# Score matmuls of two softmax passes mixed in half quads, and softmax sums inverted as [128, 32] through DRAM

## The chip, the cores and the metric

The kernel is one program on one core of a Trainium2 chip. The core has five engines that run side by side, each through its own list of instructions in order: PE (TensorE) multiplies matrices out of the on-chip memory SBUF into eight PSUM banks of [128, 512] float32; DVE (VectorE), ACT (ScalarE) and POOL (GpSimd) work elementwise; SP (SyncE) here only issues DMAs. Engines wait for each other by semaphores. The metric is the time of one execution in microseconds (us) of device time. Three runs of the kernel before took 2528.41, 2529.75 and 2535.48 us, median 2529.75. One further execution was profiled; it took 2526.84 us, of which the profile's span covers 2525.1 us.

## The reference

Four batches of 1024 tokens, 256 wide, pass through six layers in float32: a mixture of experts, a causal softmax attention with 16 heads of 16, the mixture again, a feed-forward with 4-bit rounding, a linear attention, and the feed-forward again. The change lies in the softmax attention alone:

```
q, k, v  = split heads of layernorm(x) @ W_qkv.T          # 4 batches, 16 heads, [1024, 16] each
attn     = softmax(where(j <= i, q_i . k_j / 4, -inf))     # over keys j
x        = x + (attn @ v) @ W_o.T
```

The kernel computes each row's softmax in two passes: a first one finds the row's largest score, a second one computes the scores again with that maximum taken off, exponentiates them, and multiplies them by the values and by a column of ones, which gives the sum to divide by.

## The kernel before

The stage is softmax_phase, from about 380 to 1262 us of the span. It works in 16 groups of four heads (n = 0 to 15; four groups for each batch). The four heads of a group lie in four strips of 32 partitions, so that a score matmul uses 32 of PE's 128 rows and four heads can run at the same time; such a set of four is called a quad here. Each float32 matmul shows as two PE instructions in the trace, so a quad is x8.

softmax_exponentials (L822) holds a group's loop: 12 steps, 4 for the first 512 queries (qb = 0) and 8 for the second (qb = 1). Because of the causal mask the widths of the steps are 512, 384, 256, 128, then four times 512, then 512, 384, 256, 128. A step of group n does, in PE's order:

- S: a quad of transposed scores (L866) from keys kT and from less, the queries with the maximum in a spare row; ACT turns each bank into exponentials (L877, two heads to a tile ex), and on the masked steps POOL clears the upper triangle (L880).
- other work that others holds, taken out by some(): the next batch's norm, values and projections, the output projection of the batch before (L724), the transposes for less (L818, softmax_shift), the division by the sums (softmax_quotients), and in groups 13 to 15 the router of the next layer.
- M: a quad of the maxima pass for the NEXT group n + 1 (L789); DVE reduces each of its four banks, with tensor_reduce where nothing is masked (L798), else with a masked reduction (L801, into low).
- P: the products of the exponentials of the step BEFORE with the values (L836), four matmuls into one bank acc. After the last step of a block of 512 queries DVE copies acc to ys (L845), and two DMAs on SP's queue (L851) bring the numerators to yT and the sums to den, where each sum already stands in 16 equal rows.

The matmuls of S and M, and most of the other work, take their banks in turn from a pool of 7 (bank, L96); acc has the eighth bank. A matmul therefore waits until the bank that was handed out seven takes earlier has been read, by ACT if it held S, by DVE if it held M. PE's order is that of the code (manual_schedule). The orders of DVE, ACT, POOL and SP are set when the program is built, by a scheduler with estimated durations; each engine then keeps its order, so an instruction that waits holds up all behind it.

The division (softmax_quotients, L706) works on blocks of eight heads by 512 queries, of which there are 16: four reciprocals of [128, 128] of den (L712), each followed by a multiply (L713). For qb = 0 they are put into others in the middle of an odd group (late), for qb = 1 in the even group that follows. SP's queue carries, in this stage, the spreads of projected queries and keys (L770), the two DMAs of L851 and the router's stores (L351).

## Time and profile before

| what | value |
|---|---|
| median of three runs | 2529.75 us |
| profiled execution, span | 2526.84 us, 2525.1 us |
| busy: PE, DVE, ACT, POOL over the span | 90%, 69%, 40%, 26% |
| softmax groups 0 to 15 | 449.2 to 1250.7 us, 801.5 us |
| in them busy: PE, DVE, ACT, POOL | 771.5, 568.9, 373.7, 123.2 us |
| granted PE clock in them, by group | 0.82 to 1.00 |
| one step's quads at 512 wide: S, M, P | 0.96 to 1.07 us, the same, 1.00 us from start to the next start |
| four reductions of M at 512 wide (DVE) | 2.48 us |
| four exponentials of S at 512 wide (ACT) | 2.06 us |
| reciprocal [128, 128], x64 | 930 ns mean, 57.9 us |
| multiply [128, 128], x64 | 227 to 293 ns |

A busy PE is not a PE at its peak: matmuls are recorded from their issue to a modelled end, and a quad of which one member is late counts as busy throughout. So the distance from one quad's start to the next one's start is read from the timeline instead. A group's beginning is the start of its first S matmul; the groups last 42.2 to 66.5 us, the last one, which has no M, 30.7 us. In a wait line, "A <- B: t, k, m" says that A's engine sat idle for t us in all, k times, at most m us, until B had finished.

### The profile page before, as it was taken

How to read it: one execution, taken by the hardware profiler on the slowest of the kernel's cores; microseconds unless marked ns; L12 is line 12 of the kernel's file. 1: busy time of each engine (PE TensorE's matmuls, PEld its weight loads, DVE VectorE, ACT ScalarE, POOL GpSimd, SP SyncE). 2: the span in 40 equal slices, each digit the busy share in tenths (PEclk: the TensorE clock that was granted, in tenths of full speed). 3: DMA queues.
4: the chain of work that ended last, by engine and by line, in shares of the span. 5: the costliest groups of instructions: out<-in, count | busy, mean ns of one | idle time of the engine just before them, and what ended most of it. 6: DMA issues, size and time to landing. Idle time of an engine off the chain costs nothing. (4 is left out here: it accounts for less than half of the span.)

```text
span 2525.1 us, 36840 instructions
## 1 busy us (share of the span) xinstructions
PE 2274.6 (90%) x13313; PEld 1484.8 (59%) x13313; DVE 1737.0 (69%) x4753; ACT 1004.1 (40%) x2056; POOL 648.8 (26%) x772
## 2 busy tenths in 40 slices
PE   6799995999999999999869999589887999889988
PEld 5688883443343343343458888366665777656666
DVE  6456655776776786767533323799987888788886
ACT  3223331444444444443422322355542333345552
POOL 0345441211221111111134442222214444201111
PEclk9999997999999999998879999799998999989999
DMA  5333321101101011010033331110000000000000
GB/s 168 100 120 114 113 65 46 37 15 30 32 24 30 24 36 30 14 51 9 30 119 115 104 111 49 34 36 28 9 1 1 2 2 2 1 5 16 15 15 19
DMA packets 61950, 111.90 MB, mean 44 GB/s; under 512 B 15209, under 2 KB 42377, under 8 KB 56649
## 3 DMA queue, kind: packets, MB, share of 16 engines
q0 software_dynamic: 12192, 58.21, 7.3%
q1 hardware_dynamic: 47800, 46.74, 6.4%
q10 hardware_dynamic: 1776, 4.61, 0.5%
q8 instruction: 105, 1.72, 0.3%
q14 instruction: 77, 0.62, 0.1%
HBM read 70.21 MB, written 22.54 MB: 37 GB/s over the span
## 5 line engine op out<-in xcount | busy, mean ns | idle before, releaser
L877 ACT ACTIVATE ex<-bank 128x512 f32<-128x512 f32 (+3 forms) x768 | 317.7, 496 | 405.1 <-PE bank L866 398.3
L789 PE MATMUL bank<-kT,qT 32*128 32x512 f32 (+3 forms) x1536 | 281.7, 564 | 15.8 <-DMA qT<-qk 6.1
L880 POOL TENSOR_SCALAR_AFFINE_SELECT ex<-ex 128x256 f32<-128x256 f32 x256 | 103.9, 411 | 713.9 <-ACT ex L877 709.6
L568 PE MATMUL acc<-wf,gT 128*128 128x256 f32 x1184 | 261.8, 379 | 0.0
L568 PEld LDWEIGHTS acc<-wf,gT 128*128 128x128 f32 x1184 | 225.3, 190 | 30.2
L866 PE MATMUL bank<-less,kT 32*128 32x512 f32 (+3 forms) x1536 | 223.5, 557 | 16.8 <-DVE low L801 14.2
L574 DVE TENSOR_TENSOR y<-acc,xg 128x256 f32<-128x256 f32 x74 | 28.0, 419 | 303.7 <-issue 198.0
L1141 POOL TENSOR_TENSOR hq<-hv,ham 128x704 f32<-128x704 f32 x64 | 92.4, 1444 | 515.9 <-DVE std L1102 369.7
L798 DVE TENSOR_REDUCE part<-bank 128x1 f32<-128x512 f32 x256 | 160.3, 683 | 87.3 <-PE bank L789 87.3
L1193 PE MATMUL acc<-wdT,hqT 128*128 128x256 f32 x768 | 183.2, 390 | 35.0 <-DVE x L1195 33.7
L789 PEld LDWEIGHTS bank<-kT,qT 32*128 32x128 f32 x1536 | 127.8, 195 | 111.2 <-issue 45.9
L1193 PEld LDWEIGHTS acc<-wdT,hqT 128*128 128x128 f32 x768 | 146.6, 194 | 74.0 <-issue 47.4
L836 PE MATMUL acc<-ex,va 128*32 128x512 f32 (+3 forms) x1536 | 171.9, 529 | 1.1 <-DVE ys L845 0.9
L1163 PE MATMUL pairA<-wgT,xqT 128*128 128x352 f32 x512 | 169.9, 477 | 1.5 <-ACT xqT L1152 1.3
L552 PE MATMUL pairA<-xgT,w 128*128 128x256 f32 x608 | 162.4, 390 | 9.4 <-ACT xgT L542 8.7
L866 PEld LDWEIGHTS bank<-less,kT 32*128 32x128 f32 x1536 | 84.1, 195 | 145.8 <-issue 78.9
L1163 PE MATMUL pairB<-wuT,xqT 128*128 128x352 f32 x512 | 162.2, 460 | 0.4 <-DVE h L1177 0.4
L552 PE MATMUL pairB<-xgT,w 128*128 128x256 f32 x608 | 158.5, 384 | 0.0
L801 DVE CUSTOM_DVE_ANT_0 seen<-bank,mask_q,part 128x128 bf16<-128x128 f32 (+3 forms) x256 | 126.3, 547 | 36.4 <-PE bank L789 35.9
L559 ACT ACTIVATE gT<-pairA,b1s 128x256 f32<-128x256 f32 x152 | 72.0, 473 | 170.5 <-PE pairA L552 170.5
L552 PEld LDWEIGHTS pairA<-xgT,w 128*128 128x128 f32 x608 | 108.6, 192 | 37.9 <-ACT xgT L542 15.4
L801 DVE CUSTOM_DVE_ANT_0 seen<-bank,mask_q 128x128 bf16<-128x128 f32 (+3 forms) x256 | 110.9, 483 | 27.8 <-PE bank L789 24.5
(261 smaller groups left out, 4153.3 us busy)
## 6 DMA issues: line engine op xcount, KB each, us to landing
y_d<-y SPq DMA_DIRECT2D x36, 256.0 KB, 2.1
xn_d<-xn SPq DMA_DIRECT2D x16, 512.0 KB, 2.9
x<-in_x SPq DMA_DIRECT2D x8, 512.0 KB, 10.5
kT<-qk SPq DMA_DIRECT2D x32, 128.0 KB, 2.3
qT<-qk SPq DMA_DIRECT2D x32, 128.0 KB, 2.5
yT<-ys SPq DMA_DIRECT2D x32, 128.0 KB, 2.7
den<-ys SPq DMA_DIRECT2D x32, 128.0 KB, 2.9
out<-x SPq DMA_DIRECT2D x32, 128.0 KB, 1.7
```

The source lines that it names most:

```text
L552: nc.tensor.matmul(pg[:, f, :], lhsT=w1[:, k * FF + fc * P : k * FF + (fc + 1) * P], rhs=xgT[:, k, :], start=(k == 0), stop=(k == KD - 1),)
L568: nc.tensor.matmul(po[j], lhsT=gT[fc][:, bass.ts(j, P)], rhs=wf0[:, fc, :], start=(fc == 0), stop=(fc == NF - 1))
L789: nc.tensor.matmul(pss[h][:, 0:cols], lhsT=qT[rows, bass.ts(qt, P)], rhs=kT[rows, c * BLK : c * BLK + cols], start=True, stop=True,)
L798: nc.vector.tensor_reduce(parts[i][:, h : h + 1], pss[h][:, 0:cols], AX.X, ALU.max, negate=True)
L801: nc.vector.tensor_tensor_reduce(out=seen[:, 0:cols], in0=pss[h][:, 0:cols], in1=mask_q[:, BLK - cols : BLK], scale=-1.0, scalar=parts[i][ ...
L836: nc.tensor.matmul(acc[qb][bass.ts(h, 32), c0:BLK], lhsT=va[:, kt, NG * g + h, :], rhs=exs[h // 2][:, h % 2, c0:BLK], start=(kt == 0), sto ...
L866: nc.tensor.matmul(pss[h][:, c0:BLK], lhsT=kT[rows, bass.ts(kt, P)], rhs=held["less", n, qb][rows, c0:BLK], start=True, stop=True,)
L877: nc.scalar.activation(ex[:, j, c0:BLK], pss[2 * a + j][:, c0:BLK], AF.Exp, scale=0.25)
L880: nc.gpsimd.affine_select(out=ex[:, :, c0 : c0 + P], in_=ex[:, :, c0 : c0 + P], compare_op=ALU.is_ge, fill=0.0, base=0, pattern=[[0, 2], [ ...
L1141: nc.gpsimd.tensor_tensor(blocks_of(held["hq", p][:, j]), v[:, s], am[:, s].unsqueeze(2).to_broadcast([P, n, QB]), ALU.mult)
L1163: nc.tensor.matmul(pg[:, half, 0:FIH], lhsT=held["xqT", p][:, k, j, :], rhs=w[:, k, half * FIH : (half + 1) * FIH], start=(k == 0), stop=( ...
L1193: nc.tensor.matmul(po, lhsT=hqT[:, c, :], rhs=wdT[:, c, :], start=(c == 0), stop=(c == NFI - 1))
```

## The change

Two things change, both in the softmax stage.

1. A step's eight score matmuls are issued as two half quads of four. The first holds S of heads 0 and 1 and M of heads 2 and 3, in the order S0, M2, S1, M3; the second S2, M0, S3, M1. P of the step before stands between the two halves, others behind the second. The maxima pass takes its tiles in another order (all of c = 0 first, and from the last tile to the first), so that S and M of one step have the same width. softmax_shift has fixed places, after step 1 (for this group's qb = 1) and after step 8 (for the next group's qb = 0), and nothing else is done there; others start after step 1 and are paced by a running credit. Group 15 has no next group, so its half quads hold two matmuls each.
2. For 14 of the 16 blocks the sums no longer go to den in SBUF but to a DRAM tile den_d of [8, 512]. softmax_sums reads it back as few [128, 32], takes one reciprocal, stores it to DRAM (inv_d), and reads it back eight times, one row to 16 partitions each, into rden; one multiply of [128, 512] then divides yT. In code the two steps are invert and multiply. The two blocks of the last batch's second half keep softmax_quotients.

In the program as built, SP's queue has for such a block: yT, den_d, few, inv_d, eight loads of rden. On DVE the reciprocal stands three reductions behind the copy to ys; the multiply stands five reductions behind the reciprocal in odd groups, eight in most even ones. PE's order in group 7, which has no other work, reads: three half quads, P, half quad, shift, half quad, P, two half quads, P and so on; the last P of a group stands directly behind the second half quad of its own step.

```diff
@@ -609,7 +609,7 @@
...
-                maxima = softmax_maxima(wp, 0, hb, held)
+                maxima = [lambda item=item: softmax_quad(item) for item in softmax_maxima(wp, 0, hb, held)]
...
@@ -619,14 +619,18 @@
                 maxima = []
                 if n < last:
                     maxima = softmax_maxima(wp, n + 1, 0, held) + softmax_maxima(wp, n + 1, 1, held)
-                others = [lambda: softmax_shift(wp, held, n, 1)]
+                others = []
                 if n % 2 and n + 2 <= last:
                     others.append(lambda: softmax_spread(n + 2, held))
                 if g < 2 and b + 1 < NB:
                     others.append(lambda: softmax_inputs(wp, b + 1, g, held, give_back))
+                finish = []
                 if n % 2 == 0 and n:
-                    others += softmax_quotients((n - 1) // NG, (g // 2 + 1) % 2, 1, held)
+                    others.append(inverted)
+                    first, second = softmax_sums(wp, (n - 1) // NG, (g // 2 + 1) % 2, 1, held)
+                    others.append(first)
+                    finish.append(second)
                 if b > 0 and g in (0, 2):
                     out = softmax_out(b - 1, range(2 * g, 2 * g + TPB), held)
                     others += out
@@ -636,8 +640,6 @@
                         others += [lambda v=values: next(v, None)] * (KD + TPB)
                 if n % 2 == 0 and n + 2 <= last:
                     others += softmax_project(wp, n + 2, held)
-                if n < last:
-                    others.append(lambda: softmax_shift(wp, held, n + 1, 0))
...
-                late = softmax_quotients(b, g // 2, 0, held) if g % 2 else []
+                others += finish
+                late = []
                 if n == last:
-                    late += softmax_out(b, (0, 1, 2, 3), held)
+                    late = softmax_quotients(b, 1, 0, held) + softmax_out(b, (0, 1, 2, 3), held)
+                elif g % 2:
+                    first, inverted = softmax_sums(wp, b, g // 2, 0, held)
+                    late = [first]
                 softmax_exponentials(wp, n, vas[b % 2], held, maxima, others, late)
...
+    def softmax_sums(wp, b, c, qb, held):
+        def spread(d):
+            return d.rearrange("h (r c) -> (h r) c", c=8 * BLK // P)
+        def invert():
+            inv_d = dram.tile([8, BLK], F32, tag="inv_d", name="inv_d", bufs=3)
+            few = small.tile([P, 8 * BLK // P], F32, tag="few", name="few")
+            nc.sync.dma_start(out=few, in_=spread(held["den", b, c, qb]))
+            nc.vector.reciprocal(few, few)
+            nc.sync.dma_start(out=spread(inv_d), in_=few)
+            held["rden", b, c, qb] = rden = wp.tile([P, BLK], F32, tag="den", name="den", bufs=3)
+            for h in range(8):
+                nc.sync.dma_start(out=rden[h * HD : (h + 1) * HD, :], in_=inv_d[h : h + 1, :].broadcast_to([HD, BLK]))
+        def multiply():
+            yT = held["yT", b, c, qb]
+            nc.vector.tensor_tensor(yT, yT, held.pop(("rden", b, c, qb)), ALU.mult)
+        return invert, multiply
     def softmax_quotients(b, c, qb, held):
@@ -774,33 +804,37 @@
     def softmax_maxima(wp, n, qb, held):
         lo = low[qb]
         parts = {}
-        def quad(i, c):
+        def item(i, c):
             qT, kT = held["q"][n % 2], held["k"][n % 3]
             qt = qb * TPB + i
             cols = min(BLK, (qt + 1) * P - c * BLK)
-            if c < qb:
-                parts[i] = small.tile([P, NG], F32, tag="part", name="part")
-            pss = [bank([P, BLK]) for _ in range(NG)]
-            for h in range(NG):
+            def scores(h):
                 rows = bass.ts(h, 32)
+                ps = bank([P, BLK])
                 nc.tensor.matmul(
-                    pss[h][:, 0:cols],
+                    ps[:, 0:cols],
                     lhsT=qT[rows, bass.ts(qt, P)],
                     rhs=kT[rows, c * BLK : c * BLK + cols],
                     start=True,
                     stop=True,
                 )
-            for h in range(NG):
+                return ps
+            def least(h, ps):
                 if c < qb:
-                    nc.vector.tensor_reduce(parts[i][:, h : h + 1], pss[h][:, 0:cols], AX.X, ALU.max, negate=True)
-                    continue
+                    if i not in parts:
+                        parts[i] = small.tile([P, NG], F32, tag="part", name="part")
+                    nc.vector.tensor_reduce(parts[i][:, h : h + 1], ps[:, 0:cols], AX.X, ALU.max, negate=True)
+                    return
...
+            return SimpleNamespace(scores=scores, least=least)
+        return [item(i, c) for c in range(qb + 1) for i in reversed(range(TPB))]
+    def softmax_quad(item):
+        pss = [item.scores(h) for h in range(NG)]
+        for h in range(NG):
+            item.least(h, pss[h])
     def softmax_shift(wp, held, n, qb):
@@ -843,38 +885,63 @@
             if kt == last:
                 ys = wp.tile([P, BLK], F32, tag="ys", name="ys")
                 nc.vector.tensor_copy(ys, acc[qb])
-                for i, (name, bufs) in enumerate((("yT", 6), ("den", 3))):
-                    if g % 2 == 0:
-                        held[name, b, g // 2, qb] = wp.tile([P, BLK], F32, tag=name, name=name, bufs=bufs)
-                    dst = held[name, b, g // 2, qb]
-                    at = (g % 2) * 64
-                    nc.sync.dma_start(
-                        out=dst[at : at + 64, :],
-                        in_=ys.rearrange("(a two) c -> a two c", two=2)[:, i, :],
+                c = g // 2
+                detour = (b, c) != (NB - 1, 1)
+                if g % 2 == 0:
+                    held["yT", b, c, qb] = wp.tile([P, BLK], F32, tag="yT", name="yT", bufs=6)
+                    held["den", b, c, qb] = (
+                        dram.tile([8, BLK], F32, tag="den_d", name="den_d", bufs=3)
+                        if detour
+                        else wp.tile([P, BLK], F32, tag="den", name="den", bufs=3)
                     )
-        def some(n):
-            for _ in range(min(n, len(others))):
+                at = (g % 2) * 64
+                half = ys.rearrange("(a two) c -> a two c", two=2)
+                nc.sync.dma_start(out=held["yT", b, c, qb][at : at + 64, :], in_=half[:, 0, :])
+                if detour:
+                    at, half = at // HD, ys.rearrange("(j r) c -> j r c", r=32)
+                nc.sync.dma_start(out=held["den", b, c, qb][at : at + half.shape[0], :], in_=half[:, 1, :])
+        credit = [0.0]
+        def some(s):
+            for at, m, qb in ((1, n, 1), (8, n + 1, 0)):
+                if s == at and m < NB * NG:
+                    softmax_shift(wp, held, m, qb)
+                    return
+            if s < 1:
+                return
+            credit[0] += len(others) / (len(steps) - s)
+            while others and credit[0] > 0.99:
+                credit[0] -= 1
                 others.pop(0)()
         before = None
         for s, (qb, kt, c0, last) in enumerate(steps):
-            share = len(others) / (len(steps) - s)
-            pss = [bank([P, BLK]) for _ in range(NG)]
-            for h in range(NG):
-                rows = bass.ts(h, 32)
-                nc.tensor.matmul(
-                    pss[h][:, c0:BLK],
-                    lhsT=kT[rows, bass.ts(kt, P)],
-                    rhs=held["less", n, qb][rows, c0:BLK],
-                    start=True,
-                    stop=True,
-                )
+            item = maxima.pop(0) if maxima else None
             exs = []
             for a in range(2):
+                pss, least = [], []
+                for h in (2 * a, 2 * a + 1):
+                    rows = bass.ts(h, 32)
+                    pss.append(bank([P, BLK]))
+                    nc.tensor.matmul(
+                        pss[-1][:, c0:BLK],
+                        lhsT=kT[rows, bass.ts(kt, P)],
+                        rhs=held["less", n, qb][rows, c0:BLK],
+                        start=True,
+                        stop=True,
+                    )
+                    if item:
+                        other = (h + 2) % NG
+                        least.append((other, item.scores(other)))
                 ex = wp.tile([P, 2, BLK], F32, tag="ex", name="ex", bufs=4)
                 for j in range(2):
-                    nc.scalar.activation(ex[:, j, c0:BLK], pss[2 * a + j][:, c0:BLK], AF.Exp, scale=0.25)
+                    nc.scalar.activation(ex[:, j, c0:BLK], pss[j][:, c0:BLK], AF.Exp, scale=0.25)
+                for other, ps in least:
+                    item.least(other, ps)
...
                 exs.append(ex)
-            some(math.ceil(share) if share <= 1 else math.floor(share))
-            if maxima:
-                maxima.pop(0)()
-            if before is not None:
-                products(*before)
-                if before[0] == 0 and before[1] == before[3]:
-                    others += late
-            if share > 1:
-                some(math.ceil(share) - math.floor(share))
+                if a == 0 and before is not None:
+                    products(*before)
+                    if before[0] == 0 and before[1] == before[3]:
+                        others += late
+            some(s)
             before = (qb, kt, c0, last, exs)
         products(*before)
```

More of the change, by code (lines that the diff above doesn't have):

```diff
@@ L802, in quad @@
                     out=seen[:, 0:cols],
-                    in0=pss[h][:, 0:cols],
+                    in0=ps[:, 0:cols],
                     in1=mask_q[:, BLK - cols : BLK],
@@ L810, in quad @@
                 )
-        return [lambda i=i, c=c: quad(i, c) for i in range(TPB) for c in range(qb + 1)]
+            return SimpleNamespace(scores=scores, least=least)
[4 more added lines that the diff above has]
+            item.least(h, pss[h])
     def softmax_shift(wp, held, n, qb):
```

## The prediction

> **What bounds the kernel now.** I read the page's slices first, then the waits of the groups' stretch alone (449 to 1250 us), then the timeline of single steps, last the DMA issues. In the slices the stage shows PE near full and DVE at six to seven tenths, so neither row says which of them ends last.
>
> ```profile
> PE   6799995999999999999869999589887999889988
> DVE  6456655776776786767533323799987888788886
> ```
>
> The waits name three chains: exponentials wait for S, reductions wait for M, and DVE waits for the sums to land.
>
> ```profile
> ACT ex L877 <- PE bank L866: 398.3, 178, 7.7
> DVE part L798 <- PE bank L789: 80.2, 50, 5.5
> DVE den L712 <- DMA den<-ys: 31.3, 13, 3.4
> ```
>
> So PE sets the pace, and I measure what its quads lose. A step of group 0 with no other work, 512 wide:
>
> ```profile
> 484.61 1.14 PE L866 MATMUL bank<-less,kT 32*128 32x512 f32 x8
> 485.57 1.96 PE L789 MATMUL bank<-kT,qT 32*128 32x512 f32 x8
> 486.42 0.29 PEld L789 LDWEIGHTS bank<-kT,qT 32*128 32x128 f32 x2 [0.64 <-ACT ex L877]
> 487.47 1.06 PE L836 MATMUL acc<-ex,va 128*32 128x512 f32 x8
> 488.46 0.60 PE L866 MATMUL bank<-less,kT 32*128 32x384 f32 x4
> ```
>
> S goes out in 0.96 us (484.61 to 485.57) and P in 0.99; the fourth member of M needs the bank of this step's first S, whose exponential ends only at 486.4, so it starts 0.85 us late: the step takes 3.85 us for 2.91 of work. At 384, 256 and 128 wide the same wait is about 0.7, 0.65 and 0.55. Where other work stands between S and M (group 4, 671.40 S, 672.47 a projection, 674.38 M, 675.03 P) there is no such wait. The sums cost more:
>
> ```profile
> 751.43 1.76 DVE L712 RECIPROCAL den<-den 128x128 f32<-128x128 f32 x2 [1.96 <-DMA den<-ys]
> ...
> 754.74 0.69 PE L866 MATMUL bank<-less,kT 32*128 32x256 f32 x2 [1.87 <-DVE low L801]
> 755.09 2.34 PE L789 MATMUL bank<-kT,qT 32*128 32x384 f32 x8
> 757.36 1.51 PE L836 MATMUL acc<-ex,va 128*32 128x384 f32 x8
> ```
>
> DVE stands 1.96 us for the sums and then spends 5 us on four reciprocals and four multiplies between the reductions, so banks come free late.
>
> **The change part by part.** Sums are against the profiled execution, 2526.84 us; the median lies 2.9 us above it.
>
> (a) Reciprocals go. In group 6 the steps from 752.17 to 761.54 take 2.92 (S), 2.27 (M), 1.44 (P), 0.75 (S) and 2.01 us (output projection, which waits for the multiply); free of DVE they would be about 0.54, 1.43, 0.78, 0.43 and 1.06, so S to P and the projection lose some 5 us. In group 7 (timeline from 817.56) M takes 3.29 us for 1.9, the next S 2.55 for 0.96 and the next M 1.82 for 1.39, 3.4 lost in all. Seven even and seven odd blocks change: 7 x 5.0 + 7 x 3.4 = 59 us off. Bounds 45 (the odd price for nearly all) and 65.
>
> (b) The detour's own waits come. Behind the copy to ys stand, one after the other on SP's queue, yT (issue 0.47), den_d, few, then, after the reciprocal, inv_d and eight loads. None is in the trace; their landings lie between those of the nearest rows:
>
> ```profile
> y_d<-y SPq DMA_DIRECT2D x36, 256.0 KB, 2.1
> kT<-qk SPq DMA_DIRECT2D x32, 128.0 KB, 2.3
> den<-ys SPq DMA_DIRECT2D x32, 128.0 KB, 2.9
> out<-x SPq DMA_DIRECT2D x32, 128.0 KB, 1.7
> ```
>
> I take 2.1, the row that also goes to DRAM, and 0.4 for an issue (rows between 0.33 and 0.59). The reciprocal of [128, 32] I put at 0.35, between the 253 ns of a [128, 16] (L1387) and the 702 ns of a [128, 88] (L930). From the end of ys: den_d issued at 0.55, landed 2.65; few landed 4.8; reciprocal done 5.2; inv_d landed 7.3; the eighth load issued at 10.2, landed 12.3. DVE reaches the reciprocal three reductions (3 x 0.62 = 1.9 us) after ys and stands 2.9 us; in an odd group it reaches the multiply five reductions later, at 8.3, and stands 4.0. Queued behind each are the reductions that free banks; PE asks for such a bank one step later, 1.3 to 1.7 us after it would have been read. So PE loses 1.2 + 2.7, and 0.3 of backlog, 4.2 us in groups 3, 7 and 11, about half, 2.2, in 1, 5, 9 and 13, whose steps hold other work. In even groups DVE reaches the reciprocal in step 0 and stands 3.0, less 1.3 of slack 1.7 lost; the multiply, eight reductions on, is reached at about 10, stands 2.3, 1.0 lost: 2.7. Sum 3 x 4.2 + 4 x 2.2 + 7 x 2.7 = 40 us. With every landing at 1.7 the three prices are 2.5, 1.5 and 1.25: 22 us; with 2.9 and issues of 0.59 they are 8, 5 and 5: 79. The new DVE work (14 x 0.35 + 14 x 0.69 = 15 us, 0.69 from the 128x512 multiplies) is in these prices. The projections' spreads stand behind the eight loads, but are issued five steps later, so they cost nothing; were that cover gone, each would be up to 5 us late.
>
> [...]
>
> (c) Half quads. Work per step is the same; in the middle of a group the wait is too: with banks in rotation of seven, the fourth member of a first half (M3) needs the exponential of S2, the first member of the half just before it, so again 0.85 at 512. A step of the middle stays at 3.85. What differs are the ends. The last P stands right behind its own exponentials: at 128 wide S ends its exponentials and POOL its mask about 1.6 us after issue, P could go at 0.4, loss 1.2. In step 0 the two halves stand together, so M1 waits for S0, 0.85. On masked steps P waits about 0.25 each for a mask made only a half quad earlier. In a bare group (3, 7, 11) the waits add to 9.7 after and 7.6 before (0.7 + 0.65 + 0.55 + 5 x 0.85 + 0.7 + 0.65): 2.1 each. In even groups the turns taken by inverted, first and finish bring PE no work, so three steps stay bare: 2.5 each. Elsewhere 1.3. Sum 3 x 2.1 + 8 x 2.5 + 4 x 1.3 = 31 us. Bounds 10 (P never waits for a mask) and 45.
>
> (d) Group 15 has halves of two. A matmul is two passes of about 0.43 us at 512 wide whether two heads run or four, so each half takes a whole quad's time. Twelve quads of S, followed by something else than a quad, take 6 x 1.07 + 2 x (0.86 + 0.64 + 0.43) = 10.3 us from start to start (group 15's own rows), and there are now twice as many; some 0.8 lies under a wait of 0.92 us for DVE that is there already. 9.5 us, bounds 5 (ACT's 2.06 us a step hides half) and 12.
>
> (e) The rest of DVE's lateness. The groups' 801.5 us exceed work plus the exponentials' waits by 124 us (group by group, 3 to 16 us); 59 of these are (a). The other 65 (norms, router, copies) shrink, since DVE may now be later before PE feels it: in a bare step of before, M's fourth bank is issued at 1.8, readable 1.2 later, read as the last of four by 4.6, and asked for at 4.8, a slack of 0.2 us against 1.3 for half quads. I take a quarter, 16 off, bounds 0 and 32.
>
> Edits at nothing: the other order of the maxima (the same quads), POOL's masks (the same 256), softmax_shift (0.6 us of PE wherever it stands; that it covers a wait after steps 1 and 8 is in (c)), the copies and stores of the router, which lie behind the loads on SP with a group's time to spare. Nothing outside the stage changes.
>
> Sum: -59 + 40 + 31 + 9.5 - 16 = +5.5, so 2532.3 for the profiled execution and 2535 against the median.
>
> **The rivals.** *The detour decides (slower).* One mechanism: the multiply stands in DVE's list before its data can be there, for each of 14 blocks. For it: the multiply is five reductions behind a reciprocal with a store and eight loads in between. Against: den's wait today is 31.3 us and not more. With the upper price, 79 for 40, the time is 2535 + 39 = 2574. The sum passes +7.6, 0.3%, once the detour costs over 42 us, 3.0 a block, against 2.9 in my working. *DVE's relief carries (faster).* Landings of 1.7 (22), (c) at 20, (e) at 32 off: -59 + 22 + 20 + 9.5 - 32 = -39.5, so 2490 by the median. For it: 124 us of lateness against 15 of new DVE work. Against: PE keeps the exponentials' wait. *The halves do not run four abreast*, since each member now waits for another engine: half of each of 360 half quads more, 0.4 us, is about 150 us, 2680. Against it stands group 6, where members of M start between those of S, and both quads together take 2.2 us to P at 751.17:
>
> ```profile
> 749.00 1.09 PE L866 MATMUL bank<-less,kT 32*128 32x384 f32 x5
> 749.75 0.37 PE L789 MATMUL bank<-kT,qT 32*128 32x256 f32 x1
> 749.92 0.49 PE L866 MATMUL bank<-less,kT 32*128 32x384 f32 x3
> 749.97 1.27 PE L789 MATMUL bank<-kT,qT 32*128 32x256 f32 x7
> ```
>
> **How the numbers follow.** The balance above: 0.44, with its own range 2515 to 2555. Detour decides: 0.25. Relief carries: 0.27. Not four abreast: 0.04. The range runs from the relief's 2490, rounded to 2488, to 2588, where (b) stands at its upper end of 79 and (c) at 45 (2574 + 14); what lies beyond, a part of either rival and the last one, is some 0.2. A measurement of this kernel can tell about 0.3%, 7.6 us: 2522.2 to 2537.3. Of the balance I put 0.12 below, 0.14 within and 0.18 above, so faster 0.39, same 0.14, slower 0.47.
>
> **What would show it.** (a) L712 falls from x64 to x8. (b) DVE's waits name few and rden in place of den, each 2 to 4 us, 14 times. (c) bare groups of 42 to 45 us, steps of 3.85 at 512. (d) group 15 at about 40 us. Wrong would make it: landings outside 1.7 to 2.9, half quads longer than 1.07 us, or waits of kT and qT on the DMA queue behind the loads.

## The result, and the profile after

The changed kernel takes 2559.96 us (median of four runs, 2554.04 to 2566.63) against 2529.08 for the kernel before on the same chip: a ratio of 1.0123, 95% interval 1.0087 to 1.0160, 31 us slower. It lies in the predicted range (2488 to 2588), which is as wide as it is because of the rivals, but above the 2515 to 2555 that the prediction gave to its own sum. The sum had +5.5, so 25 us are not explained by it. The profiled execution took 2559.75 us with a span of 2558.0.

First the clock row of the kernel before (PEclk, in tenths of full speed), then three rows of the changed kernel. PE and DVE look much as before; the clock is a little lower where the stage ends, 8 8 7 6 in slices 18 to 21 against 9 8 8 7:

```profile
PEclk9999997999999999998879999799998999989999
...
PE   6799995999999899999959999598987999978988
DVE  6456655666666676667343323699987888788886
PEclk9999997899999999988769999799998999989999
```

The waits of the groups (us in all, times, longest), first one line of the kernel before, then the kernel after. DVE's 31.3 us for the sums have become two entries of 26.4 and 32.0, each 11 times. Its wait for unmasked maxima fell from 80.2 to 48.4 us, that for masked ones rose from 49.6 to 117.9:

```profile
DVE seen L801 <- PE bank L789: 49.6, 50, 2.4
...
ACT ex L942 <- PE bank L819: 320.4, 234, 4.9
DVE seen L835 <- PE bank L819: 117.9, 129, 3.2
DVE part L832 <- PE bank L819: 48.4, 56, 2.8
DVE yT L732 <- DMA den<-inv_d: 32.0, 11, 4.1
DVE few L724 <- DMA few<-den_d: 26.4, 11, 3.2
```

The detour of one block, in group 7: SP's queue, and then DVE.

```profile
824.02 0.48 SPq L899 DMA_DIRECT2D yT<-ys  x1
824.55 0.53 SPq L902 DMA_DIRECT2D den_d<-ys  x1
826.75 0.34 SPq L723 DMA_DIRECT2D few<-den_d  x1
828.88 0.34 SPq L725 DMA_DIRECT2D inv_d<-few  x1
830.36 3.56 SPq L728 DMA_DIRECT2D den<-inv_d  x8
```

```profile
823.31 0.68 DVE L887 COPY ys<-acc 128x512 f32<-128x512 f32 x1
824.16 1.89 DVE L832 TENSOR_REDUCE part<-bank 128x1 f32<-128x512 f32 x3 [0.16 <-PE bank L819]
828.49 0.35 DVE L724 RECIPROCAL few<-few 128x32 f32<-128x32 f32 x1 [2.45 <-DMA few<-den_d]
828.76 3.01 DVE L832 TENSOR_REDUCE part<-bank 128x1 f32<-128x512 f32 x5
835.40 0.69 DVE L732 TENSOR_TENSOR yT<-yT,den 128x512 f32<-128x512 f32 x1 [3.62 <-DMA den<-inv_d]
```

This is the predicted sequence: the reciprocal starts 4.5 us after ys (4.8 predicted), the multiply 11.4 us (12.3), DVE stands 2.45 and 3.62 us (2.9 and 4.0), with three and five reductions before and between.

By group (start of the first S to the next one's) the stage went from 801.5 to 828.6 us: groups 0 to 14 +7.4, of which 0, 4 and 8 gained 3.8, 3.9 and 3.1, the bare groups 3, 7 and 11 are nearly unchanged (43.5, 42.4, 42.3 after 43.8, 42.2, 43.8), and group 15 +19.8 (50.4 after 30.7). The windows of group 15 show that the clock takes part (columns: window and length, busy times of PE, PEld, DVE, ACT, POOL, then the granted clock, DMA share, GB/s):

```profile
1240.00:1245.00 5.00, 4.08 (x38) 1.20 (x32) 0.00 (x0) 2.27 (x9) 1.59 (x4) 1.00 0.00 0
1250.00:1255.00 5.00, 5.00 (x22) 2.22 (x22) 3.19 (x12) 0.78 (x2) 0.00 (x0) 0.50 0.00 0
1255.00:1260.00 5.00, 5.00 (x22) 1.24 (x14) 3.09 (x12) 1.39 (x3) 0.00 (x0) 0.50 0.00 0
```

PE's timeline at two places, a step of group 0 and one of group 15:

```profile
470.58 1.02 PE L930 MATMUL bank<-less,kT 32*128 32x512 f32 x2
472.11 1.12 PE L819 MATMUL bank<-kT,qT 32*128 32x512 f32 x2 [0.52 <-DVE part L832]
472.77 1.12 PE L930 MATMUL bank<-less,kT 32*128 32x512 f32 x2
473.97 2.07 PE L819 MATMUL bank<-kT,qT 32*128 32x512 f32 x2
475.97 1.94 PE L878 MATMUL acc<-ex,va 128*32 128x512 f32 x8
...
1252.05 2.08 PE L930 MATMUL bank<-less,kT 32*128 32x512 f32 x4
1254.06 1.94 PE L878 MATMUL acc<-ex,va 128*32 128x512 f32 x8
1255.92 2.08 PE L930 MATMUL bank<-less,kT 32*128 32x512 f32 x4
```

In group 15 a P of 512 takes 1.86 us from start to start (1254.06 to 1255.92) where it took 0.99 at full clock. In the clock's records of the two kernels every half-clock stretch that begins among the groups lasts a multiple of 3.41 us: 3.41, 6.83 or 10.24, and once 17.07, in group 15 of the changed kernel (1248.74 to 1265.80). As a bound, (1 - clock) x length summed over the groups is 49.6 us before and 56.8 after; 8.6 of the latter stand in group 15, none before. Some of it is waiting: PE sat idle for 1.7 us of the half-clock stretches before and for 6.1 after.

In group 0 DVE is late with the norm and what stands among it (468.28 to 475.3). The four members of a half quad then go one by one, 5.39 us for 0.96, and the granted clock is 0.50 from 473.9 to 480.7, so P behind it takes 1.94 us too.

### The profile page after: what moved, and what is told of

The parts are those of the page before. It is cut to its first block, busy times and chain, and to the rows that moved or that the text cites. A ratio compares the mean times of both kernels' runs of the same rounds, so it can differ in the third digit from the quotient of the medians.

```text
span 2558.0 us, 37164 instructions
## 1 busy us (share of the span) xinstructions
PE 2278.6 (89%) x13313; PEld 1473.1 (58%) x13313; DVE 1698.7 (66%) x4669; ACT 1019.6 (40%) x2056; POOL 650.2 (25%) x772
## 5 line engine op out<-in xcount | busy, mean ns | idle before, releaser
L942 ACT ACTIVATE ex<-bank 128x512 f32<-128x512 f32 (+3 forms) x768 | 331.6, 491 | 393.7 <-PE bank L819 320.4
L819 PE MATMUL bank<-kT,qT 32*128 32x512 f32 (+3 forms) x1536 | 434.3, 569 | 32.1 <-DVE low L835 14.9
L930 PE MATMUL bank<-less,kT 32*128 32x512 f32 (+3 forms) x1536 | 398.2, 564 | 12.3 <-DVE part L832 6.0
L930 PEld LDWEIGHTS bank<-less,kT 32*128 32x128 f32 x1536 | 147.3, 195 | 191.5 <-issue 102.5
L819 PEld LDWEIGHTS bank<-kT,qT 32*128 32x128 f32 x1536 | 167.5, 195 | 95.9 <-ACT ex L942 31.2
L878 PE MATMUL acc<-ex,va 128*32 128x512 f32 (+3 forms) x1536 | 199.4, 533 | 7.9 <-POOL ex L947 7.3
L835 DVE CUSTOM_DVE_ANT_0 seen<-bank,mask_q,part 128x512 bf16<-128x512 f32 (+3 forms) x256 | 130.0, 546 | 84.4 <-PE bank L819 83.4
L835 DVE CUSTOM_DVE_ANT_0 seen<-bank,mask_q 128x512 bf16<-128x512 f32 (+3 forms) x256 | 112.4, 485 | 46.1 <-PE bank L819 45.1
```

The source lines that it names most:

```text
L819: nc.tensor.matmul(ps[:, 0:cols], lhsT=qT[rows, bass.ts(qt, P)], rhs=kT[rows, c * BLK : c * BLK + cols], start=True, stop=True,)
L835: nc.vector.tensor_tensor_reduce(out=seen[:, 0:cols], in0=ps[:, 0:cols], in1=mask_q[:, BLK - cols : BLK], scale=-1.0, scalar=parts[i][:, h ...
L878: nc.tensor.matmul(acc[qb][bass.ts(h, 32), c0:BLK], lhsT=va[:, kt, NG * g + h, :], rhs=exs[h // 2][:, h % 2, c0:BLK], start=(kt == 0), sto ...
L930: nc.tensor.matmul(pss[-1][:, c0:BLK], lhsT=kT[rows, bass.ts(kt, P)], rhs=held["less", n, qb][rows, c0:BLK], start=True, stop=True,)
L942: nc.scalar.activation(ex[:, j, c0:BLK], pss[j][:, c0:BLK], AF.Exp, scale=0.25)
```

## The experiments

Each ratio is against runs of the kernel before on the same chip; "us" are the ratio times 2529. Times of groups and steps come from the one profiled execution of each kernel. Steps of a group are counted from 0.

**Group 15 with whole quads.**

```diff
-                for h in (2 * a, 2 * a + 1):
+                for h in range(NG) if not item and a == 0 else (2 * a, 2 * a + 1) if item else ():
...
-                    pss.append(bank([P, BLK]))
+                    ps = bank([P, BLK])
+                    (pss if item else whole).append(ps)
...
+                if not item:
+                    pss = whole[2 * a : 2 * a + 2]
```

> The changed kernel with one edit: in group 15, which has no maxima of a next group, the four score matmuls of a step go out together again, as before the change. The changed kernel took 2560 us, group 15 in it 50.5 us against 30.7 before. Theory A (halves of two): two heads take PE as long as four, so group 15 falls by 10 us; the granted clock of 0.50 that its profile shows from about 1247 to 1266 us comes from somewhere else and stays, so the time is about 2550. Theory B (the low clock comes with the doubled matmuls): both go, group 15 falls to 31 to 33 us and the time to about 2541. Rival (the group is set by ACT or DVE once others wait there): less than 4 us, 2556 or more. Groups 0 to 14 are the same program and stay within 3 us in sum.

Measured: 1.0098 (1.0072 to 1.0125). Group 15 takes 36.8 us, 13.6 less, groups 0 to 14 784.8 against 778.2 (their clock differs, one of them at 0.88 where it was 0.97). The trace speaks for theory A with part of the clock; the time, 6 us less and uncertain by about 11, does not tell A from the rival. The 6 us that group 15 still has above the kernel before have no cause shown.

**The half quads alone.**

```diff
-                    others.append(inverted)
-                    first, second = softmax_sums(wp, (n - 1) // NG, (g // 2 + 1) % 2, 1, held)
-                    others.append(first)
-                    finish.append(second)
+                    others += softmax_quotients((n - 1) // NG, (g // 2 + 1) % 2, 1, held)
...
-                    first, inverted = softmax_sums(wp, b, g // 2, 0, held)
-                    late = [first]
+                    late = softmax_quotients(b, g // 2, 0, held)
...
-                detour = (b, c) != (NB - 1, 1)
+                detour = False
```

> The changed kernel without its second part: the sums land in den again and are inverted in four [128, 128] pieces with four multiplies, everything else (half quads, order of the maxima, places of the shift) as changed. By the prediction's own terms the detour is worth -59 + 40 = -19 net, so without it the time rises from 2560 to about 2579 and L712's 64 reciprocals come back. Rival (the detour decides: its waits cost more than the reciprocals did): the time falls below 2552. Rival (half quads are late enough that DVE's reciprocals hide in them): within 8 us of 2560; then the detour gave nothing, and all 31 us come from the half quads and group 15.

Measured: 1.0214 (1.0189 to 1.0239), 54 us. So the detour is a net gain of 23 us (uncertain by 11) inside the changed kernel, as (a) and (b) had it (19), and the first part costs 54 where the prediction's terms for it (31 + 9.5 - 16) come to 24.5.

**The detour alone**, the same lines the other way round, put into the kernel before.

```diff
-                    others += softmax_quotients((n - 1) // NG, (g // 2 + 1) % 2, 1, held)
+                    others.append(inverted)
+                    first, second = softmax_sums(wp, (n - 1) // NG, (g // 2 + 1) % 2, 1, held)
+                    others.append(first)
+                    finish.append(second)
...
-                late = softmax_quotients(b, g // 2, 0, held) if g % 2 else []
...
+                elif g % 2:
+                    first, inverted = softmax_sums(wp, b, g // 2, 0, held)
+                    late = [first]
```

> The kernel before with the second part of the change alone: sums to DRAM, one reciprocal of [128, 32], eight loads and one multiply for 14 of the 16 blocks; quads, maxima and shift as before. By the prediction's terms (a) and (b): 2529 - 59 + 40 = 2510, and up to 16 less where DVE's other lateness shrinks with it. Rival (the detour decides): 2532 or more, with DVE standing over 60 us at few and rden. Rival (DVE's relief carries, the cost is all in the half quads): 2500 or less.

Measured: 0.9907 (0.9891 to 0.9924), 24 us faster. The two parts add: 54 - 24 = 30 for 31. DVE still stands long:

```profile
DVE few L725 <- DMA few<-den_d: 38.1, 12, 4.6
DVE yT L733 <- DMA den<-inv_d: 32.4, 11, 4.3
```

By the ratio that is 2505 us, within the prediction's 2494 to 2510. The first rival is out, though DVE stands 70.5 us, and so is the second, if only just (2501 to 2510 against its 2500 or less). These 70.5 us of standing cost less than the reciprocals did.

**No waits for the landings.**

```diff
-            nc.vector.reciprocal(few, few)
-            nc.sync.dma_start(out=spread(inv_d), in_=few)
+            inv = small.tile([P, 8 * BLK // P], F32, tag="inv", name="inv")
+            nc.vector.reciprocal(inv, held["ys"][:, 0 : 8 * BLK // P])
+            nc.sync.dma_start(out=spread(inv_d), in_=inv)
...
-            nc.vector.tensor_tensor(yT, yT, held.pop(("rden", b, c, qb)), ALU.mult)
+            nc.vector.tensor_tensor(yT, yT, ones_wide, ALU.mult)
```

> The changed kernel with every transfer of the detour kept, but DVE no longer waits for them: the reciprocal of [128, 32] is taken of a part of ys, which is in SBUF, and the multiply takes a constant tile of ones in place of rden, so the division by the sums is left out. It prices what DVE's standing at few and rden (26.4 + 32.0 us in the changed kernel) costs the end. By the prediction's term (b): 40 us off, 2520. Rival (the detour decides): 55 or more off, 2505 or less. Rival (DVE's waits lie beside PE's wait for the exponentials): less than 12 off, 2548 or more.

Measured: 1.0083 (1.0057 to 1.0108), 10 us less and uncertain by 11, as the last rival had it. But the edit did not do all that it should: the multiply moved up in DVE's order and now waits for the other landing behind ys, 16.1 us in 12 times, among the widest masked reductions. It prices a smaller change than meant; the runs with the late detour replace it.

**The order of the maxima alone**, in the kernel before.

```diff
-            if c < qb:
+            if c < qb and i not in parts:
                 parts[i] = small.tile([P, NG], F32, tag="part", name="part")
...
-        return [lambda i=i, c=c: quad(i, c) for i in range(TPB) for c in range(qb + 1)]
+        return [lambda i=i, c=c: quad(i, c) for c in range(qb + 1) for i in reversed(range(TPB))]
```

> The kernel before with one edit: the maxima pass takes its tiles in the new order (all of c = 0 first, from the last tile to the first), with whole quads, the old places of the other work and the old division. The half quads alone cost 53 us (a ratio of 1.0214), of which some 20 us are group 15 and 5 us the stage's beginning; about 22 us in groups 0 to 14 have no named cause yet, and my working put this order at nothing. Theory A (the order): in the first steps DVE now has four reductions of 512 wide where it had 128 and 256, so the norms and copies that stand there come on top; 15 us or more slower, ratio 1.006 or more, group 0 longer by 3 us, the first quads of the stage at half clock. Theory B (the mixing): the order alone moves the time by less than 0.3%, and group 0 stays at 48.6 us.

Measured: 1.0133 (1.0100 to 1.0165), 34 us slower: theory A, and the edit that the prediction costed at nothing. Group 4 of this run, DVE and then PE:

```profile
663.52 0.95 DVE L712 RECIPROCAL den<-den 128x128 f32<-128x128 f32 x1 [1.81 <-DMA den<-ys]
664.39 0.63 DVE L801 CUSTOM_DVE_ANT_0 seen<-bank,mask_q 128x512 bf16<-128x512 f32 x1
...
666.17 0.69 DVE L801 CUSTOM_DVE_ANT_0 seen<-bank,mask_q 128x512 bf16<-128x512 f32 x1
666.78 0.08 DVE L801 DVE_READ_ACCUMULATOR2_ANT low<- 128x1 f32 x1
666.78 1.48 DVE L332 TENSOR_TENSOR x<-x,back 128x256 f32<-128x256 f32 x4
```

```profile
665.09 0.91 PE L866 MATMUL bank<-less,kT 32*128 32x384 f32 x2 [1.58 <-DVE low L801]
665.70 2.87 PE L789 MATMUL bank<-kT,qT 32*128 32x384 f32 x8
668.50 1.94 PE L836 MATMUL acc<-ex,va 128*32 128x512 f32 x8
```

The same place in the kernel before:

```profile
644.39 0.28 DVE L801 CUSTOM_DVE_ANT_0 seen<-bank,mask_q 128x128 bf16<-128x128 f32 x1
...
645.04 0.28 DVE L801 CUSTOM_DVE_ANT_0 seen<-bank,mask_q 128x128 bf16<-128x128 f32 x1
645.26 1.68 DVE L332 TENSOR_TENSOR x<-x,back 128x256 f32<-128x256 f32 x4
```

The four reductions of step 0 take 2.4 us (664.39 to 666.78) where they took 0.9, just ahead of the norm, with the first quotient waiting in front of them. Step 1 lasts 8.26 us against 3.17, and four pieces of half clock follow. The old order gave DVE narrow reductions where PE's S is wide and the other work stands; the new one makes PE's and DVE's heavy steps the same. Part of step 1 is only work moved forward: steps 1 to 3 together take 18.0 us for 14.1, and in the even groups without a norm, where step 1 also grows to 8.3, the group changes by -4.3 to +1.7 us. In the traces the loss lies with the norms: over the six groups that hold one (0, 1, 4, 5, 8 and 9) the trace is 21.2 us longer than that of the kernel before, over the other ten 1.2 shorter.

**Half quads with the old order**, without the detour.

```diff
-        return [item(i, c) for c in range(qb + 1) for i in reversed(range(TPB))]
+        return [item(i, c) for i in range(TPB) for c in range(qb + 1)]
```

> The half quads without the detour, and with the maxima in the order of the kernel before (tile by tile, from the first to the last), so that S and M of a step have different widths; the places of the other work stay as changed. Half quads with the new order took 1.0214 of the kernel before. Theory A (the order costs): the ratio falls to 1.012 or less, groups 0 to 2 return to 149 us in sum from 158, and the stage begins at about 449 us. Theory B (the mixing costs, whatever the order): 1.018 to 1.025, groups 0 to 14 within 5 us in sum. Group 15, which has no M, stays at 50 us in both.

Measured: 1.0254 (1.0212 to 1.0297). Neither theory: it is no better than with the new order. Groups 0 to 14 took 816 us in this trace against 793 with the new order. So each of the two costs alone (34 and 64 us), and together less than their sum (54). In the half quads the new order does not cost; it may gain, 10 us in time with an uncertainty of 12, and 23 in these two traces. So half quads seem to want equal widths.

**The same with the old beginning of the other work.** In this run the spread of later queries (issued in step 0) comes ahead of the shift that reads the old ones, so part of the scores is made of other queries; the instructions are the same in number.

```diff
-        credit = [0.0]
+        credit = [1.0]
...
-            if s < 1:
-                return
```

> As the run with half quads, old order and no detour, and the other work may again start in step 0 (the credit starts at one), so that the norm of the next batch is put out at DVE a step earlier, where M is 128 wide, as in the kernel before. Theory A (what costs is where the norm's seven us of DVE work falls): at least 6 us less than with the old order alone, steps 4 and 5 of groups 0, 4 and 8 under 6 us. Theory B (a half quad holds S behind M, so that any lateness of DVE stops PE at once): within 5 us of it, the loss only moves to another step.

Measured: 1.0210 (1.0156 to 1.0265). Step 5 of groups 0, 4 and 8 falls from 10.8, 5.7 and 5.0 to 5.4, 4.5 and 4.5 us, and other steps grow; 11 us less in time with an uncertainty of 18. It settles nothing.

**The detour, late.** Load, reciprocal with its store and loads, and multiply apart, the last two pinned to their place in the code.

```diff
+        def load():
+            held["few", b, c, qb] = few = small.tile([P, 8 * BLK // P], F32, tag="few", name="few")
+            nc.sync.dma_start(out=few, in_=spread(held["den", b, c, qb]))
...
-            nc.vector.reciprocal(few, few)
+            few = held.pop(("few", b, c, qb))
+            tc.keep_in_program_order(nc.vector.reciprocal(few, few))
...
-            nc.vector.tensor_tensor(yT, yT, held.pop(("rden", b, c, qb)), ALU.mult)
+            tc.keep_in_program_order(nc.vector.tensor_tensor(yT, yT, held.pop(("rden", b, c, qb)), ALU.mult))
...
-                    others.append(inverted)
-                    others.append(first)
+                    others += [load, inverted, invert]
...
-                    late = [first]
+                    late = [load, invert]
```

> The kernel before with the detour, whole quads, and the detour's two DVE instructions moved behind their data: the load of few, the reciprocal with its store and eight loads, and the multiply are three pieces, put a step or more apart, and reciprocal and multiply keep their place in the code. The detour alone took 0.9907 of the kernel before, with DVE standing 70.5 us at few and rden. By term (b) of the prediction DVE's standing there costs two thirds of its length, so with less than 20 us of it left the ratio falls by some 0.013, to 0.978. Rival (with whole quads this standing lies in slack, since PE's next S and the other work do not wait for it): 0.987 to 0.991. Rival (the detour alone already lies at what PE's work and the exponentials' wait allow, and a later multiply delays the output projection): 0.991 or more.

Measured: 0.9778 (0.9745 to 0.9811), 2465.6 us against 2524.6: 56 us faster than before and the fastest of all. The standing fell from 70.5 us to 17.7:

```profile
DVE few L727 <- DMA few<-den_d: 12.8, 5, 4.1
DVE yT L735 <- DMA yT<-ys: 3.1, 1, 3.1
DVE yT L735 <- DMA den<-inv_d: 1.8, 1, 1.8
```

So 52.8 us less of standing go with 33 us (uncertain by 9), 0.6 each, close to the two thirds of (b). In the traces 4.7 of them lie ahead of group 0, where the two kernels are the same. The clock has a part in the gain of the whole detour, but hardly in this step: the bound on what it takes is 49.6 us before, 18.4 with the detour alone and 16.9 here, where all groups but 0, 9, 13 and 14 run at 1.00.

**The changed kernel with the late detour**, the same edit.

> The changed kernel with the detour's two DVE instructions behind their data, as in the run of that kind with whole quads: load of few, reciprocal with store and loads, and multiply are three pieces a step or more apart, and reciprocal and multiply keep their place in the code. With whole quads this took the ratio from 0.9907 to 0.9778. Theory A (DVE's standing costs the same in both): the changed kernel's 1.0123 falls by 0.012, to 1.000, and the bare groups 3, 7 and 11 to 40 us. Rival (the half quads' own waits lie over it, as the run without landing waits suggests, which came to 1.0083): 1.005 or more.

Measured: 1.0005 (0.9986 to 1.0024): theory A. Bare groups 41.6, 40.3 and 40.3 us.

**And whole quads in group 15**, the two edits together.

> The same, and in group 15 the four score matmuls of a step go out together again. Whole quads in group 15 alone took 1.0123 to 1.0098 in the time and group 15 from 50.4 to 36.8 us in the trace. Theory A (both edits repair separate places): 13 us, 0.005, under the run with the half quads of group 15, so 0.995 if that stands at 1.000. Rival (group 15's loss is only handed to the router steps behind it, which wait for DVE): less than 6 us, 0.002, between the two.

Measured: 0.9939 (0.9916 to 0.9962), 17 us less; group 15 takes 39.6 us for 49.4, in this trace at a clock of 0.80, so 10 us show there, and the uncertainty of the time is 8.

**Late detour and the new order**, whole quads.

> The kernel with whole quads and the late detour, which took 0.9778, with the new order of the maxima. The order alone took 1.0133 of the kernel before. Theory A (the order costs by itself: DVE has four reductions of 512 wide in the steps where norms and copies stand, and none to do in the last ones): the same 0.013 on top, 0.991. Theory B (it costs by meeting the quotients, which the detour has taken away): 0.984 or less.

Measured: 0.9860 (0.9833 to 0.9886), 21 us above the late detour: between the theories. Part of the order's 34 us may have come from meeting the quotients (and DVE's load from them); the difference of 13 us is uncertain by 14. Most is its own. In the two traces 12.1 us of it lie in the six groups with a norm, -0.1 in the other ten, and 6.5 ahead of group 0.

**What a late DVE costs.** The late detour with extra reciprocals on a tile of ones.

```diff
                     late = [load, invert]
+                    if n % NG == 3:
+                        late.append(lambda: burn(2 ** ((n + 1) // NG)))
...
+    def burn(k):
+        for _ in range(k):
+            tc.keep_in_program_order(nc.vector.reciprocal(held_ones[0], held_ones[0]))
```

> The kernel with whole quads and the late detour, and in the bare groups 3, 7 and 11, where DVE has room, two, four and eight further reciprocals of [128, 128] on a tile of ones, in one place of the second half of each group (0.93 us each: 1.9, 3.7 and 7.4 us of DVE work that nobody reads). Without them these groups take 38.9, 39.6 and 39.0 us at a granted clock of 1.00. It measures what a late DVE costs. Theory A (a small slack, then one for one): +1 in group 3, +3 in group 7, +6 in group 11. Theory B (a stall of PE also costs the clock: a stretch at 0.50 follows, one or more pieces of 3.41 us, as it shows at groups 3 and 11 of the kernel before): less than 1 in group 3 and no half clock; group 11 at +8 or more, with half clock in it. Rival (a whole step of DVE's idle time takes it up): under 2 in groups 3 and 7.

Measured: 0.9830 (0.9753 to 0.9907) from two runs, which does not tell it from the late detour; the trace does. Groups 3, 7 and 11 take 39.0, 43.1 and 45.6 us, +0.2, +3.5 and +6.6. Groups 1, 2, 6, 8, 9 and 12 are the same to 0.1; the others, with nothing added, differ by +1.2 to +2.1 or by -4.6 and -3.1 (groups 13 and 14), so the reading rests on what the timeline shows in the three groups. The windows of the three groups, then the two of 3.4 us at the stall in group 7 (columns as above):

```profile
592.00:631.10 39.10, 38.99 (x304) 17.59 (x300) 28.98 (x88) 19.71 (x48) 6.42 (x16) 1.00 0.08 19
777.70:820.90 43.20, 41.71 (x304) 17.52 (x300) 31.30 (x92) 19.82 (x48) 6.42 (x16) 0.96 0.06 17
972.30:1017.90 45.60, 43.07 (x301) 17.90 (x297) 34.17 (x96) 19.81 (x48) 6.42 (x16) 0.93 0.07 16
...
804.70:808.10 3.40, 2.03 (x14) 1.11 (x10) 3.08 (x10) 1.87 (x4) 0.41 (x1) 1.00 0.10 29
808.10:811.50 3.40, 3.40 (x15) 0.30 (x10) 2.67 (x4) 0.30 (x1) 0.41 (x1) 0.50 0.03 5
```

The timeline there, with the added work on DVE and then PE:

```profile
802.38 3.90 DVE L747 RECIPROCAL ones<-ones 128x128 f32<-128x128 f32 x4
...
806.65 0.69 PE L915 MATMUL bank<-less,kT 32*128 32x512 f32 x1 [1.37 <-DVE low L844]
807.46 2.31 PE L832 MATMUL bank<-kT,qT 32*128 32x512 f32 x7
809.70 1.94 PE L879 MATMUL acc<-ex,va 128*32 128x512 f32 x8
```

Two reciprocals, 1.9 us, cost 0.2. Two more, in another group, cost 3.3 on top for 1.9 of work: PE stands 1.4 us, the piece of 3.4 us with that stall is followed by one at half clock, and P takes 1.94 us. Eight cost 6.6 us with two such pieces; they do not stand together on DVE (five, then three between reductions). Theory A has the sum but not the slack, theory B the first group and the clock, but not the 8 us.

## Why the prediction was right or wrong

Five of the runs make a chain in which one edit at a time leads from the kernel before to the changed one. The uncertainty of each difference is 8 to 11 us.

| edit | ratio from, to | measured, us | predicted, us |
|---|---|---|---|
| reciprocals go, detour late | 1, 0.9778 | -56 | (a) -59 |
| new order of the maxima | 0.9778, 0.9860 | +21 | nothing |
| half quads, with the places of P, of the shift and of other work | 0.9860, 0.9939 | +20 | (c) + (e) 31 - 16 = 15 |
| half quads in group 15 | 0.9939, 1.0005 | +17 | (d) 9.5 |
| the detour's own waits | 1.0005, 1.0123 | +30 | (b) 40 |
| sum | 1, 1.0123 | +31 | +5.5 |

(a) was right in size, in part by luck. The measured edit still contains 18 us of standing and the new DVE work. From the kernel before to the late detour the even groups 2 to 14 fell by 5.0 us on average, the odd ones 1 to 13 by 3.8, for 5.0 and 3.4; the bare groups 3, 7 and 11 by 4.9, 2.6 and 4.8, where 3 and 11 had a piece of half clock before and 7 had none. But the price of 5.0 was misread. Of group 6's loss only the 2.4 us of the first S are PE's wait for DVE. The other 2.8 were counted on quads that ran at a clock of 0.50, from 755.58 to 762.41 in the record of the kernel before, and the output projection did not wait for the multiply: PE was busy all through it. That time came back too, but with the clock, which the prediction does not name.

(b) was right in mechanism, landings, length and order. The 30 us in the half quads (33 with whole quads) price the standing alone; the new DVE work, which its 40 also hold, stays in the first row, so the size is neither confirmed nor refuted. The price by groups was wrong: bare groups lose 2 us (43.5, 42.4, 42.3 against 41.6, 40.3, 40.3), not 4.2. The working let PE lose all of each wait but 1.3 to 1.7 us. The transfers that the detour waits for took 1.5 to 2.2 us from issue to use in group 7, for the 2.1 taken.

(c) holds where it was worked out: middle steps of 3.91 us (3.85 predicted), bare groups 1.2 us longer than with whole quads (40.3 against 39.1 with the order and the late detour) for 2.1 predicted. The half quads do run four abreast: 0.96 us from 822.96 to 823.92 in group 7 of the changed kernel.

(e) rests on a slack that the runs contradict. It took whole quads to have a slack of 0.2 us and half quads 1.3, so DVE's lateness would weigh less. Two reciprocals on top, 1.9 us, cost a whole-quad group 0.2 us (with the late detour), so its slack there is about 1.7; and the half quad of group 0 shown above holds S behind M, so that it takes 5.4 us. No run took (e) by itself. Against the 15 us of the pair, the 20 measured are no clear miss (uncertain by 9), and in the two traces 16.3 of the 24.5 us lie in groups 0 to 14; the other 8.1 lie in group 15, whose quads are whole in both, at a clock of 0.80 against 0.97, with no cause shown.

(d) had the doubled matmuls right (group 15 +19.8 us, 8.6 of them the bound on its clock, so about 11 for 9.5), but not the clock. A clock of 0.82 to 1.00 by group stood in the table of before, and no term names it.

The term that decided is the sentence "Edits at nothing: the other order of the maxima (the same quads)". PE's quads are the same, DVE's work in a step is not: the order moves 1.5 us of reductions per step 0 ahead of the norms. In this chain it is worth 21 us of the 25 that the sum missed. That is its price among whole quads. Among half quads the old order was no better (1.0254 against 1.0214), so going back to it would not repair the changed kernel; what the sum missed is that order and half quads together cost 41 us for 15. So none of the rivals took place as told: the detour decides needs a detour that loses, and it is a gain of 23 us inside the changed kernel, its waits costing 30; the relief is real but was paid back elsewhere; and the balance's own sum missed the order. That the time lies in the stated range is the range's width and not the sum. The start of group 0, 454.2 us after 449.2, is charged to nothing. It lies between 453.1 and 455.2 in all kernels with the new order, which also holds for the maxima ahead of group 0, and at 449.6 or less in four of the six with the old one; but at 453.4 in the detour alone, which changes nothing ahead of it. So how much of it is the order's stays open.

Of what should show: (a) holds in the eight reciprocals left; (b)'s waits are there, 11 times each at 2.4 and 2.9 us on average; (c)'s 42 to 45 us hold; (d)'s 40 us do not.

## What to carry to other kernels

When two passes share a loop, look at what a reordering does to each engine in each step, not at the total: pairing PE's widest step with DVE's widest cost 34 us by itself, about as much as all the detour's waits. An instruction that waits for a chain of transfers belongs behind them in its engine's order; moving two instructions per block later made a gain of 24 us one of 56. And an edit that looks like one change should be priced in its separable parts: here one part won and three lost, and two of the three cost less together than apart.

## What the runs showed of the hardware

With the extra reciprocals a stall of PE was paid twice. In group 7, after a piece of 3.4 us in which PE was busy only 2.0, the granted clock was 0.50 for 3.4 us, and 1.9 us of DVE work beyond the slack cost 3.3. It is not a strict rule of the recorded busy time. Over the softmax groups of the traces before and after, pieces of 3.41 us at full clock with less than 2.1 us of busy PE were followed by half clock 14 times in 15, with 2.1 to 2.5 us 6 times in 13, and with more than 3.35 us 2 times in 294. The bound on what the clock takes in the groups is 49.6 us before, 56.8 after, 80.9 with the order alone, and 16.9 in the fastest kernel. How much of each kernel's time is the clock's and how much the waits' that bring it down, no run separates.

The transfers of few and inv_d move 16 KB each, 128 B for each of 128 partitions: in group 7 few landed 1.74 us after its issue began (826.75 to 828.49) and inv_d 1.48 (828.88 to 830.36), less than the 2.1 taken. The queue's issues were the longer part: eight loads took 3.56 us.
